# A new start for a four-layer graph kernel: order of the first loads, shape of the weight chunks, who does the one-time work, and the ranks of the matmuls

## The chip, the cores and the metric

The kernel runs on one core of a Trainium2 chip (trn2). The metric is the device time of one execution in microseconds (us), as the median of several runs. The engines are named as the profile names them: PE is the tensor engine (PEld its weight loads), DVE the vector engine, ACT the scalar engine, POOL the general engine, SP the engine that here only starts transfers. ACT can start transfers on a queue of its own as well.

## The reference

There are 128 batches of x with shape [128 nodes, 512 features] in float32, one common matrix adj [128, 128], and four layers. Each ends in a residual sum and a normalization over the 512 features.

```python
x = ln(x + max over m of relu(adj @ x [n] + b_n - (adj@x)[n] + (adj@x)[m]))   # layer 0; both weights are adj
q, k, v = x @ Wq + bq, x @ Wk + bk, x @ Wv + bv                               # layer 1: 8 heads of 64
x = ln(x + softmax(q k^T / 8 + (1 - adj) * -1e9) @ v @ Wo + bo)
h = x @ W;  e = leaky_relu(h a1 [n] + h a2 [m]) * adj                         # layer 2
x = ln(x + elu(softmax(e) @ h + beta * h))
x = ln(x + norm_adj @ (x @ weight) + bias)                                    # layer 3
```

In layer 0 the sum of adj @ x cancels but for a maximum over the features of a row, so one product A = adj @ x, a row maximum R and the bias b give it. Six products of a 128-row batch with a 512 x 512 matrix remain in layers 1 to 3: Q, K, V, Y (Wo), U (W) and Z (weight).

## The kernel before, in words

**Products.** The six products are made for a pair of batches at a time (256 rows), each by seven half-size products in place of eight (`seven_steps` writes the steps, `seven` the code). A product n has four weight combinations nT0 to nT3, made once at the start by subtractions of quarters of the weight (L699), four sums of the moving operand nS1 to nS4 (POOL, L716, for each pair), and the seven products nP1 to nP7 (PE, L737). In the profile px, py and pz are the three PSUM banks of a product: `px_V<-wv_sb,xT` is a half-product of V that reads the plain weight, `py_Q<-SX_V,QT` one that reads a sum and a combination.

**Layers.** For each batch: LD loads x (SP), ST0 takes its statistics (DVE, L640), A is adj @ x (PE, `ps_a`, L854), R the row maximum (DVE). Q0 (ACT), P0 (POOL, a power, L667) and AP0 (ACT, L671 and L672) are the normalization, in which L671 scales the shift and L672 applies scale and shift to 128 x 512 values. MX1 writes the result to a DRAM scratch dx. For batches from 4 on, MX2 reads it back in blocks of 32 rows (`xB`) and TX turns these on DVE into xT, the moving operand of Q, K and V. The first four batches don't go by way of DRAM: PX copies x into the block layout (DVE), PT turns it on PE against an identity (`ps_x`, L909), PTE copies it to xT (DVE). SC are the scores (`ps_s`), MX to SMN the softmax (L975, L981, L990, L995), O the product with v, OE its copy; then Y, the layer's second half; L and E to GE layer 2 (`ps_gT` is the turned mixture of nodes, L1034 its copy gT, on ACT); U, and so to NX, Z and OUT in layer 3.

**One-time work.** BQ scales the bias bq, MASK makes the mask of the softmax, LOG makes W a1 and W a2 (eight DVE products of 128 x 512 with a sum, L602, in one step), ROW a row of biases, NORM the normalized adj of layer 3. The weights come as four chunks of 256 KB each. wq, bq, bk and b0 are loaded from ACT's queue and all others from SP's (the list FETCH). `weight` loads chunks of 128 rows; `turned_weight`, used for Wq, Wk and Wv, loads chunks that land on 32 of the 128 partitions.

**Order.** All of these are entries of a table STEPS. Each has an engine, a cost, the steps that it follows, and the buffers that it takes with the steps that release them (POOLS holds how many buffers there are of a name). `list_order` goes through the table before the program is built and writes out one order. Among the steps that can start on PE it takes the one with the lowest `rank`, which is the batch number plus a constant of the step, the table LAG, less a correction for single pairs, the table LEAD. On other engines `soon` and `rush` put a step ahead. The engines then run their own list in that order, with semaphores between them. So a queue (of ACT, DVE, POOL, SP) is in order: what waits holds up all that stands behind it.

The lines of the profile that are spoken of most are:

```python
                (nc.vector if n in "QK" else nc.gpsimd).tensor_tensor(x, y, z, ALU.subtract)   # L699, nT0 to nT3
...
        return t, [(t[q * S : (q + 1) * S], v[q]) for q in range(Q)]                           # turned_weight
```

Of the kernel before, what the change touches and what calls it, by code (L numbers as in the profile page):

```python
# [172 lines left out]
def normed(b):  # L173
# [12 lines left out]
    "BQ": Step("DVE", 0.2, ("ADJ1", 3.0), batches=first),  # L186
    "MASK": Step("DVE", 0.5, "R", batches=first),
    "ROW": Step("PE", 3.5, "BV", "BO", takes={"ps": ("ROW1",)}, batches=first),
    "ROW1": Step("DVE", 0.7, "ROW", batches=first),
    "LOG": Step("DVE", 5.7, "BETA", "A1", batches=first, port=True),  # L190
    "LOG1a": Step("PE", 0.45, "LOG", takes={"ps": ("LOG2a",)}, batches=first),
    "LOG1b": Step("PE", 0.45, "LOG", takes={"ps": ("LOG2b",)}, batches=first),
    "LOG2a": Step("DVE", 0.65, "LOG1a", batches=first),
    "LOG2b": Step("DVE", 0.65, "LOG1b", batches=first),
    "NORM": Step("DVE", 1.2, "MASK", batches=first, port=True),
    "NORM1": Step("PE", 0.2, "NORM", takes={"ps": ("NORM2",)}, batches=first),
    "NORM2": Step("DVE", 0.3, "NORM1", batches=first),
    "LD": Step("SP", 0.4, ("LD-1", 0.0), ("LD-2", 8.0), takes={"x": ("MX1", "PX")}, dma=(2.55, 0.9)),
    "ST0": Step("DVE", 0.82, "LD", takes={"t0": ("AP0+",)}, rush=40),
    "ADJ": Step("PE", 0.2, ("LD", 2.3), takes={"ps": ("ADJ1",)}, batches=first),  # L200
# [5 lines left out]
    "AP0": Step("ACT", 1.03, "P0+", soon=20, rush=40),  # L206
    "MX1": Step("SP", 0.4, "AP0", ("MX1-1", 0.0), takes={"dx": ("MX2+", "RL")}, dma=(1.55, 0.9), rush=40),

    "PX": Step("DVE", 0.6, "AP0", takes={"xB": ("PT",)}, soon=20, batches=early, port=True, rush=40),
    "PT": Step("PE", 0.5, "PX", takes={"ps": ("PTE",)}, batches=early),  # L210
# [49 lines left out]
    "WK0 WK1 WK2 WK3 WV0 WV1 WV2 WV3 WO0 WO1 WO2 WO3 BV BO W20 W21 W22 W23 A0 A1 BETA W30 W31 W32 W33 B3"  # L260
).split()
for i, name in enumerate(FETCH):
    after = (FETCH[i - 1], 1.0 if i < 8 else 3.0) if i else ("LD@", 2.0)
    STEPS[name] = Step("SP", 0.4, after, batches=first, dma=(2.5, 0.9 if name[0] == "W" else 0.1))
for i in range(4):
    after = ((f"WQ{i - 1}", 0.4),) if i else ()
    STEPS[f"WQ{i}"] = Step("ACT", 0.1, *after, batches=first, dma=(2.5, 0.9))
# [14 lines left out]
def seven_steps(n, sums, needs, weights, pool, out, add=(), turned=False, copy=False, T="POOL"):  # L282

    def step(name, engine, cost, *after, takes=(), soon=0.0):
        after = [(sums if a[0] == "S" else n) + a if isinstance(a, str) else a[0] for a in after]
        STEPS[n + name] = Step(engine, cost, *after, takes=takes, soon=soon, batches=even if sums == "X" else paired)  # L290

    needs = [(a,) for a in needs]
    for i in range(4):
        after = [f"{n}T{i - 1}"] if i else weights
        cost = 1.34 if T == "POOL" else 0.75
        STEPS[f"{n}T{i}"] = Step(T, cost, *after, batches=first, port=True)
    parts = [n + p for p in ("P1", "P2", "P3", "P4", "P5", "P6", "P7")]
    parts += [f"{sums}S{i}" for i in (1, 2, 3, 4)] + [n + "F1"] * (sums != "X")
    for s in STEPS.values():
        s.takes = {  # L300
            p: (*r, *(q + "+" for q in parts)) if p == pool else r for p, r in s.takes.items()
        }
    last = {"R2": add, "U3": turned, "C21": True}
    last = n + next(k for k in last if last[k])
    c = 0.893 if turned else 0.866
    step("P1", "PE", c, "S1", *needs, takes={
        "ps": (n + "C11",), "u": (last,), **({"uL": (n + "C21",)} if turned else {}), **out
    })
    step("P6", "PE", c, "S2", "P1", (n + "T2@",), takes={"ps": (n + "C21",)})
    step("P5", "PE", c, "S1", "P6", takes={"ps": (n + "C12",)})  # L310
    step("P2", "PE", c, "u", *(("uL",) if turned else ()))
    step("P7", "PE", c, "S3", "U2")
    step("P4", "PE", c, "U3", (n + "T3@",))
    step("P3", "PE", c, "S4", "C22")
    added, low = "u", "uL" if turned else "u"
    if add:
        step("R1", "POOL", 0.75, "u", *((a,) for a in add), soon=20)
        step("R2", "POOL", 1.3, "R1", soon=20)
        added = low = "R2"
    step("u", "ACT", 0.42 if turned else 0.3, "P1", soon=20)  # L320
    if turned:
        step("uL", "ACT", 0.42, "P1", soon=19)
    step("U2", "DVE", 0.37, "P6", "R1" if add else "u", soon=20)
    step("U3", "DVE", 0.37, "P7", added, soon=20)
    if copy or turned:
        step("C11", "ACT", 0.42 if turned else 0.3, "P2", soon=10)
    else:
        step("C11", "DVE", 0.37, "P2", "R1", soon=10)
    step("C21", "DVE", 0.37, "P4", low, soon=10)
    step("C22", "DVE", 0.37, "U3", "P5", soon=10)  # L330
    step("C12", "DVE", 0.37, "U2", "P3", soon=10)
    return [n + c + "+" for c in ("C11", "C12", "C21", "C22")]
# [6 lines left out]
for n, needs, letters in (  # L339
# [4 lines left out]
    "Q": seven_steps("Q", "X", ["TX+", "PTE+", "BQ@"], ["WQ3"], "xT", {"qT": ("SC+",)},  # L344
                     turned=True, T="DVE"),
    "K": seven_steps("K", "X", ["TX+", "PTE+", "BQ@"], ["WK3"], "xT", {"kT": ("SC+",)},
# [3 lines left out]
    "U": seven_steps("U", "U", ["GE+"], ["LOG", "W23"], "gT", {"x3": ("OUT+",)}, copy=True),  # L350
    "Z": seven_steps("Z", "Z", ["NE+"], ["W33"], "nx", {}, add=["C3+"]),
}
for n, need, weights, end, out in (
# [16 lines left out]
    "A": 0.692, "QP4": 9.305, "QP6": 13.674, "KP4": 14.013, "QP1": 14.257, "VP6": 14.264,  # L370
    "QP7": 14.272, "KP7": 14.275, "QP2": 14.757, "KP6": 14.810, "QP5": 16.139,
    "KP1": 16.167, "SC": 16.245, "QP3": 16.292, "KP5": 16.483, "KP2": 16.726, "KP3": 16.957,
    "VP1": 17.469, "VP7": 17.505, "VP2": 17.717, "VP4": 17.842, "VP3": 17.872,
    "VP5": 17.926, "YP4": 18.786, "YP5": 19.034, "O": 20.374, "YP3": 21.316, "YP1": 21.809,
    "YF1": 21.819, "YP2": 21.908, "YP6": 21.936, "YP7": 22.056, "E": 22.106, "UF1": 22.207,
    "YF0": 22.911, "BT": 23.043, "UP1": 23.223, "GT": 23.299, "UP4": 23.974, "UP5": 24.264,
    "UP3": 24.731, "UP2": 24.753, "UP6": 24.814, "UP7": 24.920, "UF0": 25.326,
    "ZP7": 25.453, "ZF0": 25.880, "NX": 25.925, "ZP4": 26.433, "ZP2": 26.459, "ZP6": 26.533,
    "ZP1": 27.158, "ZP3": 27.371, "ZP5": 27.563, "ZF1": 28.500,
}  # L380

LEAD = {
    "V55": -0.01, "NX59": 0.02, "GT60": -2.5, "V60": 0.06, "BT61": 0.07, "Z61": -1.43,
    "BT62": -0.59, "GT63": 1.52, "NX63": -0.85, "A4": 3.8, "O0": 1.06, "O1": -0.73, "GT2": 0.02,
    "V1": -0.26,
# [6 lines left out]
def rank(name, b):  # L392
    if name not in LAG:
        return -1.0
    stage = name[0] if name[1:2] in "PF" else name
    if name in ("SC", "O") and b in BOTH:
        b |= 1
    return b + LAG[name] - LEAD.get(f"{stage}{b // 2}", 0.0)


@with_exitstack
def kernel(
# [61 lines left out]
    nc.scalar.dma_start(out=b0_sb, in_=b0.rearrange("(p o) -> p o", o=1))  # L464
# [3 lines left out]
    def LD(b):  # L468
        xs[b] = buf("x", [P, D], b)
        nc.sync.dma_start(out=xs[b], in_=x[b])  # L470
# [5 lines left out]
    def turned_weight(w, name):  # L476

        t = const.tile([P, C, D], F32, tag=name, name=name)
        v = w.rearrange("(q c s) f -> q s c f", q=Q, s=S)
        return t, [(t[q * S : (q + 1) * S], v[q]) for q in range(Q)]  # L480
# [8 lines left out]
    def row(v, offset, size, name):  # L489
# [19 lines left out]
        *wk_parts, *wv_parts, *wo_parts, bv_part, bo_part, *w2_parts, *a_parts, beta_part, *w3_parts,  # L509
# [10 lines left out]
    for part in (bq_part, bk_part):  # L520
        fetch(nc.scalar, part)
# [18 lines left out]
    prep = {}  # L540

# [15 lines left out]
    def NORM():  # L557
# [5 lines left out]
        nc.vector.tensor_scalar(dis, deg, TINY, None, op0=ALU.max)  # L563
        nc.gpsimd.tensor_tensor(dis, dis, neg_half, ALU.pow)
        nc.vector.tensor_tensor(dis, dis, pos, ALU.mult)
# [30 lines left out]
    def LOG():  # L596
        nc.vector.tensor_scalar(beta_id, ident, beta_c, None, op0=ALU.mult)
        for i in range(2):
            col = prep[i] = tiny(f"wa_col{i}", 0, C)
            for c in range(C):  # L600
                prod = buf("m", [P, D], f"prod_{i}_{c}")
                nc.vector.scalar_tensor_tensor(  # L602
                    prod,
                    w2_sb[:, c, :],
                    1.0,
                    a_bc[i],
                    op0=ALU.mult,
                    op1=ALU.mult,
                    accum_out=col[:, c : c + 1],
                )  # L610
# [58 lines left out]
    def apply(dst, src, layer, b):  # L669
        shift, scale = off[layer, b // 2][:, b % 2], rstd[layer, b // 2][:, b % 2]  # L670
        nc.scalar.activation(shift, shift, AF.Identity, scale=scale)  # L671
# [226 lines left out]
    def PX(b):  # L898
        xB[b] = buf("xB", [P, Q, P], b)
        nc.vector.tensor_copy(  # L900
            xB[b].rearrange("p c (q s) -> p c q s", s=S),
            xs[b].rearrange("p (q c s) -> p c q s", q=Q, s=S),
        )
# [307 lines left out]
    def OUT(b):  # L1211
# [5 lines left out]
        LD, ST0, A, R, P0, AP0, MX1, PX, PT, PTE, MX2, RL, C1, TX, SC, M0, M, SM1, EXP, SMR, SMN, MS1, MS2, TS, O, OE,  # L1217
        Y1, P1, AP1, L, E, EZ, E1, EE, E2, BT, BE, GT, GE, U1, UE, U2, UP, U3, P2, AP2, NX, NE,
        C3, Z1, P3, AP3, OUT,
    )}  # L1220
    for name in FETCH:
        do[name] = lambda b, part=parts[name]: fetch(nc.sync, part)
    for f in (ADJ, ADJ1, BQ, MASK, NORM, NORM1, NORM2, ROW, ROW1, LOG):
        do[f.__name__] = lambda b, f=f: f()
# [3 lines left out]
    for i in range(4):  # L1228
        do[f"WQ{i}"] = lambda b, i=i: fetch(nc.scalar, wq_parts[i])
# [47 lines left out]
```

## Time and profile before

| | |
|---|---|
| median of three runs | 3055.86 us (3053.38 to 3056.80) |
| span of the profiled execution | 3055.6 us (its own time is not given apart from it) |
| PE busy, idle | 3021.9 us, 33.7 us |
| DVE, ACT, POOL busy | 2350.8, 2215.0, 1624.7 us |
| first product with a weight (px_Q) starts | 24.52 us |
| first half-product of K starts | 46.49 us |
| 600 to 2900 us: PE busy | 2297.58 of 2300 us |

A row of the timeline reads: start and duration in us, engine, line, operation, output and inputs by the program's names, tile, shape, how many alike were put together, and in brackets the idle time of the engine just before it with what ended it. A row of the windows reads: the stretch in us and its length, busy us of each engine with the number of instructions, then the granted clock of PE (1.00 is full speed), the mean busy share of the 16 DMA engines, and what they moved in GB/s. The chain of waits follows the work that ended last back to its releasers.

### The profile page before, as it was taken

Reading aid. Unit: us, or ns where it says so; the run is one execution under the profiler, and the core shown is the slowest. Engines: PE = TensorE matmul, PEld = TensorE weight load, DVE = VectorE, ACT = ScalarE, POOL = GpSimd, SP = SyncE. Lnnn points to the kernel's source line nnn. Section 1 sums busy time; section 2 is a strip of 40 time slices with the busy share of each in tenths; the row PEclk is TensorE's granted clock in tenths of the full one; section 3 lists DMA queues with packets and bytes.
Section 4 is the critical chain, followed back from the end, with each engine's and each line's share of the span. In section 5 each row is a group of like instructions: output and inputs, shape, how many; then the busy total and the mean of one; then the engine's idle time right before and its main releaser. Section 6 shows DMA issues by size and latency. Waiting matters only on the chain.

```text
span 3055.6 us, 61911 instructions
## 1 busy us (share of the span) xinstructions
PE 3021.9 (99%) x21062; PEld 2706.8 (89%) x21062; DVE 2350.8 (77%) x5379; ACT 2215.0 (72%) x7240; POOL 1624.7 (53%) x1907
## 2 busy tenths in 40 slices
PE   7999999999999999999999999999999999999998
PEld 5888988988989989989889899898898898999987
DVE  6878777787787787877777877878778777777774
ACT  4677777777777776777777777777777777667675
POOL 4336555455455555554554655545545545556544
PEclk8999999999999999999999999999999999999999
DMA  7523333233233332332332323323323333223221
GB/s 198 179 87 124 89 107 111 85 116 104 84 118 98 97 114 88 111 108 83 118 102 91 117 88 107 111 87 115 104 84 118 98 97 109 86 77 97 70 84 38
DMA packets 235276, 313.19 MB, mean 102 GB/s; under 512 B 27729, under 2 KB 157649, under 8 KB 234961
## 3 DMA queue, kind: packets, MB, share of 16 engines
q1 hardware_dynamic: 233184, 308.19, 31.9%
q8 instruction: 167, 2.74, 0.4%
q10 hardware_dynamic: 1776, 1.05, 0.2%
q14 instruction: 149, 1.21, 0.1%
HBM read 174.92 MB, written 134.22 MB: 101 GB/s over the span
## 4 chain that ended last, share of the span: by engine, by line
PE 94%; DVE 3%; DMA 2%; ACT 1%; issue 0%; SPq 0%; POOL 0%; ACTq 0%; POOLq 0%; DVEq 0%
PE py_Q L737 6%; PE py_K L737 5%; PE py_U L737 5%; PE py_Y L737 5%; PE py_V L737 5%; PE py_Z L737 5%; PE ps_s L945 4%; PE pz_Q L737 4%; PE px_K L737 4%; PE pz_K L737 4%; PE ps_o L1024 4%; PE ps_nx L1181 4%; PE px_Q L737 4%; PE ps_gT L1130 4%; PE px_Z L737 4%; PE pz_V L737 4%
## 5 line engine op out<-in xcount | busy, mean ns | idle before, releaser
L1195 POOL TENSOR_TENSOR x<-x,b_bc 128x512 f32<-128x512 f32 x128 | 162.8, 1273 | 601.7 <-PE ps_nx L1181 601.6
L672 ACT ACTIVATE x<-x,off,rstd 128x512 f32<-128x512 f32 x512 | 416.8, 814 | 17.1
L981 ACT ACTIVATE s<-s,mx 128x128 f32<-128x128 f32 x1024 | 396.1, 390 | 36.7 <-DVE mx L975 36.6
L640 DVE BATCH_NORM_STATS2 st<-x 128x6 f32<-128x512 f32 x512 | 346.6, 677 | 13.9 <-POOL x L1162 7.7
L995 ACT ACTIVATE s<-s,sm 128x128 f32<-128x128 f32 x1024 | 313.3, 389 | 18.5 <-DVE sm L990 7.8
L667 POOL TENSOR_TENSOR rstd<-rstd,neg_half 128x2 f32<-128x2 f32 (+1 forms) x265 | 182.3, 688 | 149.9 <-ACT rstd L653 149.7
L1162 POOL TENSOR_TENSOR x<-x,x 128x512 f32<-128x512 f32 x128 | 163.2, 1275 | 142.4 <-DVE rs L1108 75.4
L716 POOL TENSOR_TENSOR SX_V<-xT 128x256 f32<-128x256 f32 x128 | 93.7, 732 | 272.2 <-PE py_Y L737 243.8
L1034 ACT COPY nx<-ps_nx 128x512 f32<-128x512 f32 x128 | 74.9, 585 | 215.9 <-PE ps_nx L1181 215.6
L1066 DVE SCALAR_TENSOR_TENSOR junk<-x,wa_bc 128x512 bf16<-128x512 f32 x256 | 207.1, 809 | 14.8 <-ACT x L672 4.0
L796 DVE TENSOR_TENSOR x<-py_U,u_U 128x256 f32<-128x256 f32 x183 | 77.6, 424 | 151.8 <-PE py_U L737 151.3
L981 ACT ACTIVATION_READ_ACCUMULATOR s<-s,mx 128x1 f32 x1024 | 193.5, 189 | 0.0
L959 DVE TENSOR_TENSOR s<-ps_s,mask 128x512 f32<-128x512 f32 x256 | 169.1, 682 | 9.3 <-DMA dp<-s 5.8
L896 POOL TENSOR_TENSOR x<-x,bo_bc 128x512 f32<-128x512 f32 x128 | 160.3, 1274 | 14.5 <-DVE bo_bc L593 8.1
L716 POOL TENSOR_TENSOR S_U<-gT 128x256 f32<-128x256 f32 x122 | 93.0, 762 | 128.8 <-ACT gT L1034 128.6
L1016 DVE STREAM_TRANSPOSE sB<-sB 128x1024 f32<-128x1024 f32 x128 | 157.9, 1234 | 0.8 <-DMA sB<-dp 0.8
L737 PEld LDWEIGHTS px_K<-xT,wk_sb 128*128 128x128 f32 x1024 | 133.8, 192 | 27.3 <-issue 23.6
L671 ACT ACTIVATE off<-off,rstd 128x1 f32<-128x1 f32 x512 | 145.6, 284 | 15.4 <-POOL rstd L667 15.2
L975 DVE TENSOR_REDUCE mx<-s 128x8 f32<-128x1024 f32 x128 | 153.5, 1199 | 0.3
L945 PE MATMUL ps_s<-kT,qT 64*128 64x128 f32 x2048 | 148.8, 285 | 0.0
L945 PEld LDWEIGHTS ps_s<-kT,qT 64*128 64x128 f32 x2048 | 124.3, 187 | 23.4 <-issue 23.1
L854 PE MATMUL ps_a<-x,adjT 128*128 128x512 f32 x256 | 134.4, 609 | 6.5 <-DMA x<-in_x 6.5
(190 smaller groups left out, 9151.1 us busy)
## 6 DMA issues: line engine op xcount, KB each, us to landing
dp<-s SPq DMA_DIRECT2D x128, 512.0 KB, 2.9
sB<-dp SPq DMA_DIRECT2D x512, 128.0 KB, 3.1
x<-in_x SPq DMA_DIRECT2D x128, 256.0 KB, 3.4
dx<-x SPq DMA_DIRECT2D x128, 256.0 KB, 4.4
x<-dx SPq DMA_DIRECT2D x64, 512.0 KB, 4.0
out_x<-x SPq DMA_DIRECT2D x128, 256.0 KB, 2.0
xB<-dx SPq DMA_DIRECT2D x496, 64.0 KB, 2.0
wo_sb<-in_L_gnn_Wo SPq DMA_DIRECT2D x5, 256.0 KB, 3.7
```

What stands on the lines that cost most here:

```text
L640: nc.vector.bn_stats(st, t)
L667: nc.gpsimd.tensor_tensor(r, r, neg_half.to_broadcast([P, r.shape[1]]), ALU.pow)
L672: nc.scalar.activation(dst, src, AF.Identity, bias=shift, scale=scale)
L716: nc.gpsimd.tensor_tensor(s[:, i], x, y, op)
L737: nc.tensor.matmul(to, lhsT=one, rhs=two, start=(new and k == 0), stop=(k == 1), skip_group_check=True,)
L945: nc.tensor.matmul(scores[b][par][:, c, :], lhsT=qT[b][rows, c, cols], rhs=kT[b][rows, c, cols], start=True, stop=True,)
L959: nc.vector.tensor_tensor(by_head(probs[b])[:, par * C : (par + 1) * C], scores[b][par].rearrange("p h (q s) -> p h q s", s=S), mask.rearr ...
L981: nc.scalar.activation(s[:, :, h], s[:, :, h], AF.Exp, bias=mx[:, h : h + 1], accum_out=sums[b][:, h : h + 1],)
L995: nc.scalar.activation(s[:, :, h], s[:, :, h], AF.Identity, scale=sm[:, h : h + 1])
L1066: nc.vector.scalar_tensor_tensor(junk, x2[b][:, b % 2], 1.0, wa_bc[i], op0=ALU.mult, op1=ALU.mult, accum_out=s12[b][:, i : i + 1],)
L1162: nc.gpsimd.tensor_tensor(t, t, x2.pop(b)[:, b % 2], ALU.add)
L1195: nc.gpsimd.tensor_tensor(t, t, b3_bc, ALU.add)
```

## The change

What it does, part by part:

- **First loads.** x_0 is loaded from ACT's queue with b0 behind it, and x_1 from SP's. The chunks of wq and the biases bq and bk move from ACT's queue to SP's, where the order is now adj, x_1, wq (4), bq, x_2, x_3, wk (4), bk, wv (4), dx_0, dx_1, wo (2), x_4, and so on. A load of x is released by MX1 alone.
- **Weight chunks.** A chunk of `turned_weight` is now one c for all q and s, so that it lands on all 128 partitions (2 KB each); before it was one q, on 32 partitions (4 times 2 KB each).
- **Layout copy.** PX is gone. For batches 0 to 3 ACT applies the normalization to x twice: once straight into the block layout (AB), then in place (AP0).
- **Identity turns.** 44 turns of the identity into a scores bank that nobody reads: WU0 (12) ahead of adj's turn, WU1 (14) after A of batch 1, WU2 (10) after A of batch 3, WU3 (8) after PT of batch 1.
- **One-time work.** LOG is split into one small step and eight, NORM into three with its power on POOL, BQ waits for its own load and MASK stands behind PTE; Q's and K's combinations follow other steps.
- **Ranks.** LAG has new constants, with two further tables, EARLY for the batches below 8 and LATE for those from 120; LEAD is gone.

```diff
-    "BQ": Step("DVE", 0.2, ("ADJ1", 3.0), batches=first),
-    "MASK": Step("DVE", 0.5, "R", batches=first),
+    "BQ": Step("DVE", 0.2, "BQL", batches=first, rush=60),
+    "MASK": Step("DVE", 0.5, "PTE+", batches=first),
...
-    "LOG": Step("DVE", 5.7, "BETA", "A1", batches=first, port=True),
-    "LOG1a": Step("PE", 0.45, "LOG", takes={"ps": ("LOG2a",)}, batches=first),
-    "LOG1b": Step("PE", 0.45, "LOG", takes={"ps": ("LOG2b",)}, batches=first),
+    "LOG": Step("DVE", 0.2, "BETA", batches=first),
+    **{f"LOG{i}": Step("DVE", 0.72, "BETA", f"LOG{i - 1}" if i else "LOG", batches=first, port=True)
+       for i in range(8)},
+    "LOG1a": Step("PE", 0.45, "LOG3", takes={"ps": ("LOG2a",)}, batches=first),
+    "LOG1b": Step("PE", 0.45, "LOG7", takes={"ps": ("LOG2b",)}, batches=first),
...
-    "NORM": Step("DVE", 1.2, "MASK", batches=first, port=True),
-    "NORM1": Step("PE", 0.2, "NORM", takes={"ps": ("NORM2",)}, batches=first),
+    "NORM": Step("DVE", 0.7, "QC12", batches=first),
+    "NORMP": Step("POOL", 0.58, "NORM", batches=first),
+    "NORMA": Step("DVE", 0.5, "NORMP", batches=first, port=True),
+    "NORM1": Step("PE", 0.2, "NORMA", takes={"ps": ("NORM2",)}, batches=first),
...
-    "LD": Step("SP", 0.4, ("LD-1", 0.0), ("LD-2", 8.0), takes={"x": ("MX1", "PX")}, dma=(2.55, 0.9)),
+    "LD": Step("SP", 0.4, ("LD-1", 0.0), ("LD-2", 2.0), takes={"x": ("MX1",)}, dma=(2.55, 0.9)),
...
-    "ADJ": Step("PE", 0.2, ("LD", 2.3), takes={"ps": ("ADJ1",)}, batches=first),
+    "WU0": Step("PE", 2.4, takes={"sc": ("WU0",)}, batches=first),
+    "WU1": Step("PE", 1.6, ("A", 0.0), takes={"sc": ("WU1",)}, batches=lambda b: b == 1),
+    "WU2": Step("PE", 1.1, ("A", 0.0), takes={"sc": ("WU2",)}, batches=lambda b: b == 3),
+    "WU3": Step("PE", 0.9, ("PT", 0.0), takes={"sc": ("WU3",)}, batches=lambda b: b == 1),
+    "ADJ": Step("PE", 0.2, ("LD", 2.3), "WU0", takes={"ps": ("ADJ1",)}, batches=first),
...
-    "AP0": Step("ACT", 1.03, "P0+", soon=20, rush=40),
+    "AB": Step("ACT", 1.1, "P0+", takes={"xB": ("PT",)}, soon=20, batches=early, rush=80),
+    "AP0": Step("ACT", 1.03, "P0+", "AB", soon=20, rush=40),
...
-    "PX": Step("DVE", 0.6, "AP0", takes={"xB": ("PT",)}, soon=20, batches=early, port=True, rush=40),
-    "PT": Step("PE", 0.5, "PX", takes={"ps": ("PTE",)}, batches=early),
+    "PT": Step("PE", 0.5, "AB", takes={"ps": ("PTE",)}, batches=early),
...
-    "WK0 WK1 WK2 WK3 WV0 WV1 WV2 WV3 WO0 WO1 WO2 WO3 BV BO W20 W21 W22 W23 A0 A1 BETA W30 W31 W32 W33 B3"
+    "WQ0 WQ1 WQ2 WQ3 BQL WK0 WK1 WK2 WK3 BKL WV0 WV1 WV2 WV3 WO0 WO1 WO2 WO3 BV BO W20 W21 W22 W23 A0 A1 BETA W30 W31 W32 W33 B3"
...
-    step("P1", "PE", c, "S1", *needs, takes={
+    step("P1", "PE", c, *([] if sums == "X" else ["S1"]), *needs, takes={
...
-    "Q": seven_steps("Q", "X", ["TX+", "PTE+", "BQ@"], ["WQ3"], "xT", {"qT": ("SC+",)},
+    "Q": seven_steps("Q", "X", ["TX+", "PTE+", "BQ@"], ["WQ3", "P0"], "xT", {"qT": ("SC+",)},
...
-    "K": seven_steps("K", "X", ["TX+", "PTE+", "BQ@"], ["WK3"], "xT", {"kT": ("SC+",)},
+    "K": seven_steps("K", "X", ["TX+", "PTE+", "BKL@"], ["WK3", "XS4"], "xT", {"kT": ("SC+",)},
...
-    stage = name[0] if name[1:2] in "PF" else name
-    if name in ("SC", "O") and b in BOTH:
-        b |= 1
-    return b + LAG[name] - LEAD.get(f"{stage}{b // 2}", 0.0)
+    lag = (EARLY if b < 8 else LATE if b >= 120 else LAG)[name]
+    return (b | 1 if name in ("SC", "O") else b) + lag
...
-        nc.sync.dma_start(out=xs[b], in_=x[b])
+        (nc.sync if b else nc.scalar).dma_start(out=xs[b], in_=x[b])
+        if b == 0:
+            nc.scalar.dma_start(out=b0_sb, in_=b0.rearrange("(p o) -> p o", o=1))
...
-        v = w.rearrange("(q c s) f -> q s c f", q=Q, s=S)
-        return t, [(t[q * S : (q + 1) * S], v[q]) for q in range(Q)]
+        v = w.rearrange("(q c s) f -> c q s f", q=Q, s=S)
+        return t, [(t[:, c, :], v[c]) for c in range(C)]
...
-    for part in (bq_part, bk_part):
-        fetch(nc.scalar, part)
...
+    def WU(n):
+        def step(b):
+            ps = psum.tile([P, C, P], F32, tag="sc", name=f"ps_warm_{b}", bufs=POOLS["sc"])
+            for i in range(n):
+                nc.tensor.transpose(ps[:, i % C, :], ident, ident)
+        return step
...
+    def LOG0(i, c):
+        if c == 0:
+            prep[i] = tiny(f"wa_col{i}", 0, C)
+        nc.vector.scalar_tensor_tensor(
+            buf("m", [P, D], f"prod_{i}_{c}"),
+            w2_sb[:, c, :],
+            1.0,
+            a_bc[i],
+            op0=ALU.mult,
+            op1=ALU.mult,
+            accum_out=prep[i][:, c : c + 1],
+        )
...
-    def PX(b):
+    def AB(b):
         xB[b] = buf("xB", [P, Q, P], b)
-        nc.vector.tensor_copy(
+        shift, scale = off[0, b // 2][:, b % 2], rstd[0, b // 2][:, b % 2]
+        nc.scalar.activation(shift, shift, AF.Identity, scale=scale)
+        nc.scalar.activation(
             xB[b].rearrange("p c (q s) -> p c q s", s=S),
             xs[b].rearrange("p (q c s) -> p c q s", q=Q, s=S),
+            AF.Identity, bias=shift, scale=scale,
         )
```

The three rank tables in full are of no use to a reader; as examples, KP2 goes from 16.726 to 18.942, UF1 from 22.207 to 37.454 and ZF0 from 25.880 to 8.142 in LAG.

## The prediction

> **What bounds the kernel now.** I read the page's rows of busy time first, then the windows (after the stretch: busy us of each engine, TensorE's granted clock, DMA share, GB/s), then TensorE's timeline with its waits, last the chain.
>
> ```profile
> span 3055.6 us, 61911 instructions
> PE 3021.9 (99%) x21062; PEld 2706.8 (89%) x21062; DVE 2350.8 (77%) x5379; ACT 2215.0 (72%) x7240; POOL 1624.7 (53%) x1907
> ...
> PEclk8999999999999999999999999999999999999999
> ```
> TensorE works in all but 33.7 us of the span.
> ```profile
> 0.00:10.00 10.00, 4.20 (x5) 1.29 (x5) 4.50 (x15) 1.99 (x5) 0.81 (x9) 1.00 0.78 162
> 10.00:20.00 10.00, 2.40 (x3) 0.64 (x3) 2.30 (x8) 2.64 (x7) 1.23 (x2) 0.60 1.07 227
> 20.00:30.00 10.00, 7.04 (x25) 4.66 (x25) 8.18 (x19) 4.02 (x12) 5.08 (x7) 0.72 0.69 232
> 30.00:40.00 10.00, 7.96 (x36) 6.27 (x37) 8.98 (x13) 2.78 (x11) 6.25 (x7) 0.83 0.76 224
> ...
> 600.00:2900.00 2300.00, 2297.58 (x16188) 2072.21 (x16188) 1789.72 (x4094) 1691.66 (x5525) 1260.22 (x1478) 1.00 0.32 100
> ```
> From 600 to 2900 us only 2.4 of 2300 us are idle, so nothing can be won there; the same row shows what could be lost. The loss lies in the first 40 us, where the clock was 0.60 to 0.83 besides.
> ```profile
> 16.87 2.07 PE L854 MATMUL ps_a<-x,adjT 128*128 128x512 f32 x2 [5.18 <-DMA x<-in_x]
> ...
> 24.52 1.57 PE L737 MATMUL px_Q<-xT,wq_sb 128*128 128x128 f32 x8
> 25.93 1.03 PE L737 MATMUL px_V<-wv_sb,xT 128*128 128x256 f32 x4
> ...
> 46.49 1.05 PE L737 MATMUL px_K<-xT,wk_sb 128*128 128x128 f32 x8
> ...
> 89.54 1.22 PE L737 MATMUL py_Q<-SX_V,QT 128*128 128x128 f32 x8 [2.31 <-DVE qT L789]
> ```
> The start waits for x_2 behind the weights; the first weight product starts at 24.52. Up to 46.49 TensorE does 8 A (ps_a, 0.86 each warm), 4 turns of x (0.45), 7 half-products of Q (0.89), 5 of V (0.87) and adjT (0.2), 19.45 us at full clock. So **the start loses 46.49 - 19.45 = 27.0 us**. A second loss is at 89.54: 2.31 us of idling and, with clocks of 0.61 and 0.54 in the two windows behind it, about 1.7 more. The DVE timeline ahead of it shows eight LOG products (L602) in one block from 82.29 to 88.98, with qT behind them. The tail after the last matmul is 7.2 us.
>
> **The change part by part.** The profiled execution's span, 3055.6, stands 0.26 below the median of 3055.86, which I ignore beside a spread of 3.4.
>
> *Multiset.* Matmuls stay 10,672, plus 44 idle turns of the identity; runs of one matmul form go from 270 to 268. So TensorE's full-clock work is unchanged, and only stalls and clock differ.
>
> *Weight chunks over 128 partitions (decides most).* What rows show of the two shapes:
> ```profile
> 6.00:8.00 2.00, 2.00 (x4) 0.61 (x2) 1.47 (x4) 0.00 (x0) 0.00 (x0) 1.00 1.07 200
> 84.00:86.00 2.00, 2.00 (x9) 1.15 (x8) 1.90 (x7) 1.66 (x8) 0.00 (x0) 1.00 1.05 396
> ```
> With all engines full, chunks on 32 partitions move 200 GB/s and loads on 128 partitions 396. By these rows the new chunk of 256 KB takes 0.66 us instead of 1.3. [...] Four engines move 4 x 396/16 = 99 GB/s: 2.65 us a chunk, 12 chunks 32 us on the same four engines, and whatever stands behind them on SP waits there. [...]
>
> *Start, four engines.* SP now issues adj, x_1, wq0-3, bq, x_2, x_3, wk0-3, bk, wv0-3, dx_0, dx_1, wo0, wo1, x_4. adj and x_1 are through near 4.4; wq lands at 7.1, 9.8, 12.4, 15.1; x_2 and x_3 at 16.1 and 16.8 (each about 0.66 on 16 engines); wk ends at 27.5; wv1 lands at 33.2 and wv3 at 38.6; dx_0 39.3, x_4 42.05. DVE's BQ and the four QT sums (0.69 each, L699 of the chain) need all of wq and stand ahead of PTE, done 19.5. TensorE: A2 and A3 at low clock to 19.6, the turns to 21.8, px_Q at 22.8 (before 24.52). Next in its order is px_V, which needs wv0 and wv1: **it stops from 23.7 to 33.2**. Then Q, V and two turns go on at low clock, A4 starts at 43.0 with x_4, and A5 ends at 44.8. By then 6 A, 4 turns, 7 Q, 2 V and adjT, 15.1 us of full-clock work, are done: loss 29.7, **+2.7** on before.
>
> *Queues moved past.* ACT loses six DMA issues and gains one (x_0); SP gets five more ahead of x_2. On ACT the copy of px_V (u_V) now stands ahead of AB2 and AB3, so they start at 34.2 and end near 37.5; the turns of x_2 and x_3 wait for them, ahead of A4's 43.0, hence no further cost. On POOL the four VT sums wait for wv3 at 38.6 and hold S sums of the second pair only. MX1 alone now releases x: x_4 takes the buffer that dx_0 frees, itself behind wv at 39.3, and is ready 2.75 later, after dx_1, wo0 and wo1, as counted above.
>
> *Start, sixteen engines.* wq is there by 7 and the path is x_2, R, AB, PT, PTE: px_Q near 14.5, A5 ends at 25.4 to 26.4: loss about 11, **-16**.
>
> *AB on ACT for PX on DVE.* Takes four copies (3.2 us in sum) from DVE; ACT pays 0.81 and 0.28 a batch, the rows of L672 and L671, in a stretch where its windows show 2.6 to 4 of 10 us busy. Counted in the walk. AP0 comes after AB and only dx waits for it, which no product needs before TX of batch 4. LD 0 on the ACT queue starts as early as before; b0 behind it is first read after A0.
>
> *44 turns.* At most 0.28 each (the eight of 20.77 took 2.25 at low clock), 12 us in groups of 12, 14, 10 and 8, all in stretches in which TensorE waits for x_0, x_2, AB and PTE. Cost 0; if all these covers went, 0.11 to 0.28 each, 5 to 12 us. As for the clock, the row has 0.60 to 0.72 from 10 to 30 us. [...] In the four-engine case px_V waits anyhow; in the other the difference is about 1.7 us, within its range.
>
> *LOG in eight pieces, MASK and NORM later.* The 6.7 us block goes, and the 2.31 + 1.7 behind it: **-4.0**. What is late next there is DVE itself, 18.8 of 20 us busy from 80 to 100, so up to 2 could come back. In exchange DVE at 43 to 48 has st_4, st_5, R4, R5, deg and two KT sums ahead of V's and K's additions: **+1.5** (0 to 3). NORM's pow on POOL is one 0.69 piece and only NORM1 waits for it.
>
> *Ranks.* EARLY and LATE order the two ends, LAG the middle. LATE ends pair 126 whole ahead of 127: **-0.5** (-1.4 to 0) of the tail. EARLY puts O_0 20.3 us of matmuls behind SC_0, the softmax chain needing 18.2, and similar tight places: **+1** (0 to 3). In the middle the order is almost that of before, with one difference: px_U comes 3 matmul steps (2.7 us) behind ps_gT instead of 6.
> ```profile
> 1429.27 2.45 ACT L995 ACTIVATE s<-s,sm 128x128 f32<-128x128 f32 x8
> 1431.62 0.56 ACT L1034 COPY gT<-ps_gT 128x512 f32<-128x512 f32 x1
> ...
> 1432.26 0.73 POOL L716 TENSOR_TENSOR S_U<-gT 128x256 f32<-128x256 f32 x1 [2.41 <-ACT gT L1034]
> ...
> 1435.27 1.03 PE L737 MATMUL px_U<-w_sb,gT 128*128 128x256 f32 x4
> ```
> The copy waited for ACT's softmax block, S_U ended at 1432.99 and px_U came 2.3 us later; walked in the new order the slack is about 1.1. Cost **0**; below nothing is excluded, since only 2.4 us are idle there, and above nothing is the third case.
>
> Sum, four engines: 3055.6 + 2.7 + 1.5 - 4.0 - 0.5 + 1.0 = 3056.3, with the 0.26 **3056.5** (3049 to 3064).
>
> **The rivals.** *Sixteen engines:* -16 - 4.0 - 0.5, +1 to +2: **3038** (3033 to 3045). For it: the row of 396 GB/s for loads on 128 partitions. [...] *The middle stalls (slower):* in the order S_U then px_U the slack of 1.1 us is exceeded whenever ACT starts its 2.45 us block just before ps_gT ends. From a delay of 1.1 on, TensorE waits once a pair; a mean of 0.3 over some 55 pairs is +16: **3072** (3062 to 3085). For it: ACT is 1691.66 of 2300 us busy, and blocks of eight go uninterrupted. Against it: before has places with like slack and idles 2.4 us in 2300. *It does not do what it says:* the early loads are late behind slow chunks; that is the forecast itself, and why a prologue made to be shorter is here not.
>
> **How the numbers follow.** Four engines 0.70, sixteen 0.15, stalls in the middle 0.13, others 0.02. 0.2% (6.1 us) is about what a measurement of this kernel tells from no change: bounds 3049.7 and 3062.0. Faster: all of sixteen and 0.10 of the first, 0.25. Slower: all of stalls, 0.14 of the first and the others, 0.25 together. Same: 0.50. The range 3038 to 3070 leaves out half of the second and of the third case and little else, about 0.17. The likeliest case alone holds 3049 to 3064.
>
> **What would show it.** Right: weight chunks landing about 2.65 us apart; DMA share near 0.25 to 0.4 up to 38 us; TensorE idle over 8 us ahead of the first px_V, released by wv_sb; no idle of 2 us behind LOG; the 600 to 2900 window still above 2297 busy. Wrong: px_V within 2 us of px_Q and px_Q before 17 (sixteen engines); or over 10 us of idle ahead of px_U or S_U between 600 and 2900, released by gT (stalls).

## The result, and the profile after

The changed kernel takes 3093.68 us (median of 4 runs, 3091.88 to 3096.09) against 3056.33 us: a ratio of 1.0123, interval 1.0109 to 1.0137. It is slower by 37 us. The forecast of 3056.5 was wrong, and so was its range up to 3070. The profiled execution of the changed kernel took 3091.88 us, the fastest of the four; its span is 3090.0 us, 34.4 longer than the span before. So the traces show 34.4 us of the loss, and the start that they show is that of the quickest of the four.

The page first, in the same rows as before:

```profile
span 3090.0 us, 61891 instructions
...
PE 3040.0 (98%) x21106; PEld 2706.6 (88%) x21106; DVE 2369.1 (77%) x5375; ACT 2207.7 (71%) x7244; POOL 1636.0 (53%) x1907
```

TensorE idles for 50.0 us where it idled for 33.7. Now the windows of the changed kernel (stretch, busy us of each engine, granted clock, DMA share, GB/s):

```profile
0.00:10.00 10.00, 6.55 (x31) 4.91 (x31) 3.54 (x9) 3.16 (x9) 1.52 (x10) 1.00 0.36 112
10.00:20.00 10.00, 2.31 (x3) 1.17 (x4) 2.42 (x5) 3.00 (x5) 0.00 (x0) 0.57 0.41 131
20.00:30.00 10.00, 5.37 (x36) 4.15 (x34) 6.54 (x13) 2.17 (x9) 3.48 (x5) 0.84 0.29 99
30.00:40.00 10.00, 6.71 (x31) 5.84 (x32) 0.88 (x2) 2.86 (x7) 0.00 (x0) 0.56 0.52 174
...
600.00:2900.00 2300.00, 2283.03 (x15954) 2040.01 (x15954) 1786.28 (x4043) 1663.48 (x5456) 1249.88 (x1455) 1.00 0.31 99
```

Two things are to be read here. The start is no shorter, and between 20 and 30 us the sixteen DMA engines were busy to 0.29 and moved 99 GB/s. While only weights move (18 to 20 us, for one) the share is 0.26, where it is 1.12 with the old form of the chunks (12 to 16 us of e4, below). That is about a quarter, as much as four of the sixteen engines give when they are busy all the time; no view names the engines. And the last row, which had 2297.58 us of TensorE in 2300, has 2283.03, with 234 matmuls fewer (15,954 against 16,188). The loss is in the middle.

TensorE's timeline of the start:

```profile
17.69 3.78 PE L892 MATMUL ps_a<-x,adjT 128*128 128x512 f32 x4 [8.29 <-DMA x<-in_x]
...
24.31 1.06 PE L775 MATMUL px_Q<-xT,wq_sb 128*128 128x128 f32 x8
31.59 1.20 PE L775 MATMUL px_V<-wv_sb,xT 128*128 128x256 f32 x2 [6.21 <-DMA wv_sb<-in_L_gnn_Wv]
34.48 1.22 PE L775 MATMUL px_V<-wv_sb,xT 128*128 128x256 f32 x2 [1.70 <-DMA wo_sb<-in_L_gnn_Wo]
...
44.18 1.88 PE L892 MATMUL ps_a<-x,adjT 128*128 128x512 f32 x4
```

The second px_V waits for the second chunk of wv; its row names wo, but the releaser is inferred, and the same row of e3 names wv_sb. This is the walk of the prediction to within 2 us (table further below). So where are the 34 us? The product of v (`ps_o`) of one and the same pair of batches can be found in both timelines, here of batches 6 and 7 and of batches 118 and 119, first before, then after:

```profile
231.87 1.97 PE L1024 MATMUL ps_o<-sB,v 128*64 128x128 f32 x32
2842.64 1.97 PE L1024 MATMUL ps_o<-sB,v 128*64 128x128 f32 x32
```
```profile
232.03 1.97 PE L1065 MATMUL ps_o<-sB,v 128*64 128x128 f32 x32
2877.46 1.97 PE L1065 MATMUL ps_o<-sB,v 128*64 128x128 f32 x32
```

At the first point the two profiles are 0.16 us apart, at the second 34.82. In 56 pairs 34.7 us are lost, 0.62 us in each on the mean, and the end adds -0.4. The median distance from one pair to the next is 46.69 us before and 47.35 after.

TensorE's table of waits from 600 to 2900 us, which in the changed kernel has a single row (engine and tile that waited, for what, us in total, times, longest), names the place:

```profile
PE py_Z L775 <- DVE x L834: 16.7, 49, 0.4
```

The kernel before has one row there too, another one:

```profile
PE pz_V L737 <- DVE v L796: 2.4, 4, 1.1
```

One such place in the changed kernel, first TensorE's timeline, then that of DVE:

```profile
1420.31 1.13 PE L775 MATMUL px_Z<-w_sb,nx 128*128 128x256 f32 x4
1421.27 1.03 PE L775 MATMUL py_Z<-ZT,S_Z 128*128 128x256 f32 x4
1422.14 1.03 PE L775 MATMUL px_Z<-w_sb,nx 128*128 128x256 f32 x4
1423.00 1.05 PE L1171 MATMUL ps_gT<-bT,x 128*128 128x128 f32 x8
1424.39 1.13 PE L775 MATMUL py_Z<-ZT,S_Z 128*128 128x256 f32 x4 [0.34 <-DVE x L834]
1425.36 1.03 PE L775 MATMUL px_V<-wv_sb,xT 128*128 128x256 f32 x4
```
```profile
1421.18 1.21 DVE L1016 TENSOR_REDUCE mx<-s 128x8 f32<-128x1024 f32 x1
1422.31 0.88 DVE L1199 SCALAR_TENSOR_TENSOR x<-m,x 128x512 f32<-128x512 f32 x1
1423.12 0.68 DVE L677 BATCH_NORM_STATS2 st<-x 128x6 f32<-128x512 f32 x1
1423.83 0.18 DVE L678 BATCH_NORM_AGGREGATE mv<-st 128x2 f32<-128x6 f32 x1
1423.93 0.41 DVE L834 TENSOR_TENSOR x<-py_Z,x 128x256 f32<-128x256 f32 x1
```

The second half-product py_Z (step ZP7) adds onto the bank that the DVE sum `x<-py_Z,x` (step ZU2) has to read first. That sum stands behind a maximum, an addition and statistics of other layers on DVE and ends at 1424.34. ZP7's turn was at 1423.89. In the kernel before, the same place reads:

```profile
1407.19 1.05 PE L1130 MATMUL ps_gT<-bT,x 128*128 128x128 f32 x8
1408.08 1.03 PE L737 MATMUL px_V<-wv_sb,xT 128*128 128x256 f32 x4
1408.94 1.03 PE L737 MATMUL py_V<-VT,SX_V 128*128 128x256 f32 x4
1409.81 1.03 PE L737 MATMUL py_Z<-ZT,S_Z 128*128 128x256 f32 x4
```
```profile
1408.13 0.40 DVE L796 TENSOR_TENSOR x<-py_Z,x 128x256 f32<-128x256 f32 x1
```

There the sum ended at 1408.53, and ZP7 came at 1409.81, behind two half-products of V: 1.28 us of slack. The new ranks (ZP7 from 25.453 to 1.702) put ZP7 ahead of these two, 1.73 us sooner. 1.28 - 1.73 = -0.45 us. On DVE nothing moved: from the start of px_Z to the start of the sum it is 3.64 us before and 3.62 after. The row shows 0.34 idle; the rest stands beside it, since TensorE also loses the overlap of one product with the next (the step from ps_gT to py_Z is 1.39 long, not 0.89, and that from py_Z to px_V 0.97, not 0.86).

### The profile page after: what moved, and what is told of

The parts are those of the page before. It is cut to its first block, busy times and chain, and to the rows that moved or that the text cites. A ratio compares the mean times of both kernels' runs of the same rounds, so it can differ in the third digit from the quotient of the medians.

```text
span 3090.0 us, 61891 instructions
## 1 busy us (share of the span) xinstructions
PE 3040.0 (98%) x21106; PEld 2706.6 (88%) x21106; DVE 2369.1 (77%) x5375; ACT 2207.7 (71%) x7244; POOL 1636.0 (53%) x1907
## 4 chain that ended last, share of the span: by engine, by line
PE 80%; DVE 14%; ACT 2%; issue 1%; SPq 1%; DMA 1%; POOL 0%; ACTq 0%; POOLq 0%; DVEq 0%
PE py_Q L775 5%; PE py_K L775 5%; PE py_U L775 5%; PE py_V L775 5%; PE py_Y L775 5%; PE py_Z L775 4%; PE ps_nx L1222 4%; PE pz_Q L775 4%; PE px_Q L775 4%; PE pz_K L775 4%; PE px_K L775 4%; PE pz_V L775 3%; PE pz_U L775 3%; PE px_U L775 3%; PE px_V L775 3%; PE pz_Y L775 3%
## 5 line engine op out<-in xcount | busy, mean ns | idle before, releaser
L775 PEld LDWEIGHTS py_Q<-SX_V,QT 128*128 128x128 f32 x1024 | 125.8, 193 | 31.8 <-issue 29.8
L775 PE MATMUL py_Z<-ZT,S_Z 128*128 128x256 f32 x488 | 131.3, 392 | 19.9 <-DVE x L834 19.9
L775 PE MATMUL px_V<-wv_sb,xT 128*128 128x256 f32 x512 | 133.0, 382 | 8.7 <-DMA wv_sb<-in_L_gnn_Wv 6.2
```

The costliest lines, as they stand in the source:

```text
L775: nc.tensor.matmul(to, lhsT=one, rhs=two, start=(new and k == 0), stop=(k == 1), skip_group_check=True,)
```

## The experiments

All are the changed kernel or the kernel before with the edit shown; times are medians, with the kernel before at 3055.6 to 3055.9 in the same sessions. "The written order" is what `list_order` gives; `moved` is a function put around it.

**e1: ZP7 later.** Only the place of ZP7 in the changed kernel.

```diff
+def moved(order):
+    names = [(name, b) for _, name, b in order]
+    for b in range(0, 128, 2):
+        if ("ZP7", b) not in names:
+            continue
+        i = names.index(("ZP7", b))
+        near = names[i + 1 : names.index(("ZU3", b))]
+        sixth = [k for k in near if k[0] == "VP6"]
+        if sixth:
+            names.insert(names.index(sixth[0]), names.pop(i))
+    return [(0.0, *k) for k in names]
...
-        for _, name, b in list_order(STEPS, rank, POOLS, B):
+        for _, name, b in moved(list_order(STEPS, rank, POOLS, B)):
```

> The changed kernel with one step moved in the written order: of each pair, ZP7 (the second half-product py_Z) stands behind VP1 and VP6, as in the kernel before, not ahead of them. Theory (P7 comes 1.73 us sooner than in the kernel before and so 0.45 us ahead of the DVE sum of py_Z that it waits for): the pair's period goes from 47.35 back to 46.69 us, no wait of py_Z for DVE is left, and 52 pairs of 0.66 give back 34 us: 3059 us (3054 to 3063). Rival (the new ranks cost elsewhere too, by matmuls that take longer after changes of form): less than 20 us come back, 3074 or more. Rival (the new start is what costs): nothing comes back, 3093.

Measured: 3072.12 us, ratio 1.0052 (1.0040 to 1.0065). 21.6 of the expected 34 us came back, near the border of the first rival. The wait of py_Z is gone from the table. What stays beside e3 (below) is 0.21 us a pair in the traces (46.87 from one pair to the next on the mean of batches 6 to 118, and 46.67 in e3), and the timeline shows it as a step that is too long, without a wait beside it:

```profile
1421.57 1.03 PE L788 MATMUL py_V<-VT,SX_V 128*128 128x256 f32 x4
1422.54 1.10 PE L788 MATMUL pz_Z<-w_sb,S_Z 128*128 128x256 f32 x4
1423.48 1.03 PE L788 MATMUL px_V<-wv_sb,xT 128*128 128x256 f32 x4
```
```profile
1420.85 1.24 DVE L1070 STREAM_TRANSPOSE sB<-sB 128x1024 f32<-128x1024 f32 x1
1422.01 0.39 DVE L847 TENSOR_TENSOR x<-pz_Z,x 128x256 f32<-128x256 f32 x1
```

From py_V to pz_Z it is 0.97 us and not 0.86, and the next step 0.94. pz_Z adds onto the bank that a DVE sum has to read first, and this sum ends at 1422.40, behind a transpose of 1.24. On the mean of 900 to 2300 us the two steps cost 0.18 us more a pair than in e3, some 10 us in 56 pairs. With ZP7 moved alone, the products of Z behind it are too close to their own sums. So moving this one step doesn't restore the old order, and e1 by itself leaves room for the first rival; e2 and e3 decide.

**e2: the kernel before with ZP7 earlier.** The same kind of function moves ZP7 ahead of VP1; nothing else of the change is in it.

> The kernel before with one step moved: ZP7 of each pair stands ahead of VP1 and VP6, straight behind ps_gT, as in the changed kernel. Nothing else of the change is in it. Theory (the distance of P7 from the DVE sum is enough by itself): a wait of 0.34 us in each pair, period 47.35, 58 pairs by 0.66 us: 3094 us (3088 to 3097). Rival (it needs the other ranks of the change as well): 3056 to 3060.

Measured: 3101.64 us, ratio 1.0150 (1.0136 to 1.0164). The one step suffices; it costs 46 us where 38 were expected. The table of waits has the same row as the changed kernel, 16.8 us in 49 times; the other 8 us fit two of Z's later steps, as in e1 (from py_Z<-ZT,nx to the next it is 0.97 on the mean of 900 to 2300 us, not 0.87, and from pz_Z 0.90).

```profile
PE py_Z L750 <- DVE x L809: 16.8, 49, 0.4
```

**e3: the sum earlier on DVE.** TensorE's order is that of the change; on DVE the statistics (step U3) go behind ZU2.

```diff
+        i = names.index(("ZU2", b))
+        near = [k for k in names[i - 4 : i] if k[0] == "U3"]
+        if near:
+            names.insert(i, names.pop(names.index(near[0])))
```

> The changed kernel with PE's order untouched; on DVE the sum that P7 waits for (ZU2, x<-py_Z) stands ahead of the statistics of layer 2 (U3, 0.68 and 0.18 us) in each pair. Theory (P7 is late only because ZU2 is queued behind that block on DVE): ZU2 ends 0.86 us sooner, 0.4 us ahead of P7's turn; no wait is left, period 46.7 to 46.8, 3059 us (3054 to 3066). Rival (P7 waits for something else that ends at the same time, such as the matmul P6 or POOL's sum R1): most of the wait stays, 3080 or more.

Measured: 3060.23 us (18 runs), ratio 1.0016 (1.0009 to 1.0023). 33.5 of the 37 us are back, with ZP7 as early as in the change. The DVE and PE timelines of this kernel at such a place:

```profile
1412.40 0.89 DVE L1211 SCALAR_TENSOR_TENSOR x<-m,x 128x512 f32<-128x512 f32 x1
1413.20 0.41 DVE L846 TENSOR_TENSOR x<-py_Z,x 128x256 f32<-128x256 f32 x1
1413.54 0.68 DVE L689 BATCH_NORM_STATS2 st<-x 128x6 f32<-128x512 f32 x1
```
```profile
1413.08 1.05 PE L1183 MATMUL ps_gT<-bT,x 128*128 128x128 f32 x8
1413.97 1.03 PE L787 MATMUL py_Z<-ZT,S_Z 128*128 128x256 f32 x4
```

The sum ends at 1413.61, and py_Z starts at 1413.97 without waiting. From one pair to the next it is 46.75 us (median), where it was 47.35. So P7 waited for nothing but ZU2's place in DVE's queue. What the rest of the change costs is 4.7 us in medians.

**e4: the old form of the weight chunks.** e1 with

```diff
-        v = w.rearrange("(q c s) f -> c q s f", q=Q, s=S)
-        return t, [(t[:, c, :], v[c]) for c in range(C)]
+        v = w.rearrange("(q c s) f -> q s c f", q=Q, s=S)
+        return t, [(t[q * S : (q + 1) * S], v[q]) for q in range(Q)]
```

> The changed kernel with ZP7 moved as in e1 and, besides, the chunks of Wq, Wk and Wv in the old form (32 partitions of 4 times 2 KB, 32 outermost in the source). Theory (the new form runs on four of the sixteen DMA engines, and px_V waits for wv behind eight such chunks): a chunk takes 1.3 instead of 2.5 us, wv is there by 22, px_V starts near 22 and not at 31.6 and 34.5, A4 near 33 and not at 44.2: 8 to 12 us less than e1, 3049 us (3044 to 3053). Rival (the start is bound by something else, such as SP's issuing or the chain of statistics): within 3 us of e1.

Measured: 3060.80 us (21 runs), 11.3 less than e1. The windows and the timeline show the start as expected:

```profile
12.00:16.00 4.00, 3.92 (x24) 2.57 (x23) 3.64 (x7) 2.51 (x5) 0.00 (x0) 1.00 1.12 201
```
```profile
23.02 2.05 PE L788 MATMUL px_V<-wv_sb,xT 128*128 128x256 f32 x4 [5.15 <-DMA wv_sb<-in_L_gnn_Wv]
...
33.80 1.88 PE L905 MATMUL ps_a<-x,adjT 128*128 128x512 f32 x4
```

201 GB/s at a share of 1.12 with chunks on 32 partitions, against 99 GB/s at 0.29 with chunks on 128 (20 to 30 us of the changed kernel). A4 comes at 33.80 and not at 44.18.

**e5: the kernel before with the new form of the chunks** (the two lines of e4 the other way round).

> The kernel before with the new form of the chunks of Wq, Wk and Wv and nothing else of the change. Theory (twelve chunks on four of sixteen DMA engines, 2.5 us each, some 30 us in all): px_V can start only when wv is there, near 34 us and not at 25.9, DMA share near 0.3 from 12 to 30 us: slower by 4 to 11 us, 3063. Rival (all sixteen engines, or a start bound by the statistics): within 2 us of the kernel before.

Measured: 3069.40 us, ratio 1.0047 (1.0034 to 1.0059): 13.6 us slower, more than expected. The mechanism was right, the first victim another one: not px_V, but A2, whose x stands behind weights on the same queue.

```profile
27.17 2.08 PE L854 MATMUL ps_a<-x,adjT 128*128 128x512 f32 x2 [15.94 <-DMA x<-in_x]
...
36.92 1.03 PE L737 MATMUL px_V<-wv_sb,xT 128*128 128x256 f32 x4
```

**e6: both mended.** e3's DVE order and e4's chunks in the changed kernel.

> The changed kernel with two edits: the DVE order of e3 (the sum for P7 ahead of the statistics) and the old form of the weight chunks as in e4. Theory (the two losses are independent: 33 us in the pairs, 11.3 us in the start): 3060.2 - 11.3 = 3049 us (3046 to 3052), faster than both kernels. Rival (part of the shorter start is lost again in the first pairs, which wait for something else): 3053 or more.

Measured: 3048.98 us (20 runs), ratio 0.9978 (0.9972 to 0.9985). The two losses add up as expected, and without them the change is a gain of 6.8 us.

**e7: wv ahead of wk** in FETCH, otherwise e6.

> As e6, with wv ahead of wk in SP's list. Theory (the start's next bound is the load of wv, for which px_V waited 5.2 us in e4): px_V starts near 18 and not at 23.0, A4 near 29: 4 to 6 us less than e6, 3044 us (3042 to 3048). Rival (DVE's KT sums or dx and x_4 behind the weights take the place of that wait): within 2 us of e6.

Measured: 3061.49 us (18 runs), 12.5 more than e6. px_V did start at 16.96. But FETCH feeds the planner, which wrote another order: in this one TensorE waits 4.85 us for x at 93.61 and runs at a clock of 0.83 from 80 to 100 us. It is busy for 14.05 of these 20 us, in e6 for 18.90; the rest of the 12.5 isn't placed.

```profile
93.61 3.75 PE L904 MATMUL ps_a<-x,adjT 128*128 128x512 f32 x4 [4.85 <-DMA x<-in_x]
```

**e8: four turns in place of 44** (`range(1)` in place of `range(n)`), otherwise e6.

> As e6, with four turns of the identity in place of 44 (one for each group); the order is the same. Theory (the turns lie in waits and do not hold the clock): within 1.5 us of e6, granted clock from 8 to 16 us not lower than in e6. Rival (they keep the clock up in this shorter start): the A of batches 2 and 3 and the first turns of x run at half clock (0.5 to 0.6 from 12 to 16 us), 2 to 4 us more than e6. Rival (they are in the way): 1 to 3 us less than e6.

Measured: 3046.78 us (7 runs), ratio 0.9971 (0.9961 to 0.9982), 2.2 us less than e6. The intervals of the two ratios overlap a little, so the gain isn't sure; its size is that of the second rival (they are in the way), and more than the theory allowed. The pace did change. A of batches 2 and 3 in e6, and in e8:

```profile
12.01 1.88 PE L904 MATMUL ps_a<-x,adjT 128*128 128x512 f32 x4
```
```profile
10.96 3.68 PE L904 MATMUL ps_a<-x,adjT 128*128 128x512 f32 x4 [0.73 <-DMA x<-in_x]
```

With 14 turns ahead of them the same four matmuls ran in half the time, 1.88 us for 3.68. Only these durations tell: the windows have a granted clock of 1.00 from 8 to 16 us in both runs. The other runs with the old chunks agree, 2.23 and 1.90 us with all turns (e4, e7) and 3.78 with four (e10). It bought nothing, since the turns themselves take at least what they save (the 14 take 2.00 us in e6, the four matmuls behind them 1.80 less than in e8): A2 starts later by 1.05 us in e6, px_Q starts at 16.57 in e6 and at 15.97 in e8, and then px_V waits for wv and starts at 22.29 and at 22.27.

**e9: the kernel before with LOG in pieces**, as in the diff of the change, but that the small step still waits for A1 too.

> The kernel before with LOG as one small step and eight pieces, as in the changed kernel; nothing else of the change, though the written order near that place shifts with it. Theory (the 6.7 us block on DVE cost 4.0 us at 89.54): no wait of 2 us of py_Q for qT between 80 and 95 us, 2 to 4 us less: 3052.5 us. Rival (DVE is so full there that the time comes back in other waits): within 1.5 us of the kernel before.

Measured: 3061.32 us (21 runs), ratio 1.0018 (1.0011 to 1.0024): slower by 5.4, which neither theory nor rival foresaw. From 60 to 100 us the only wait left is 0.4 us, where 2.3 stood before. But TensorE is busy for 92.79 us of the next 100, before for 98.50:

```profile
80.00:100.00 20.00, 19.57 (x151) 16.23 (x151) 19.51 (x47) 12.53 (x45) 6.19 (x5) 1.00 0.80 244
100.00:200.00 100.00, 92.79 (x680) 80.24 (x679) 76.45 (x174) 72.04 (x267) 35.24 (x44) 1.00 0.37 116
```

What was won by 100 us is lost by 200. The order near that place shifted too, so this run doesn't say how much of it is DVE's load and how much is the order.

**e10: wv ahead of wk, the order kept.** e8, with the loads of wv and wk exchanged in SP's list alone.

```diff
+    slots = [i for i, k in enumerate(names) if k[0][:2] in ("WK", "WV", "BK")]
+    loads = [names[i] for i in slots]
+    for i, k in zip(slots, [k for k in loads if k[0][:2] == "WV"] + [k for k in loads if k[0][:2] != "WV"]):
+        names[i] = k
```

> As e8 (sum for P7 earlier, old chunks, four turns), with wv ahead of wk in SP's list and every other list exactly as in e8. Theory (in e7 it was the order that the planner wrote anew for the other load that lost the time, with A waiting 4.9 us for x at 93.6; the earlier wv itself is a gain): px_V near 17, 2 to 5 us less than e8: 3043 us. Rival (KT, ahead of the first qT sums on DVE and now waiting for a later wk, gives the time back): within 1 us of e8.

Measured: 3045.09 us (3040.55 to 3045.47, 5 runs), ratio 0.9962 (0.9949 to 0.9974): 10.8 us less than the kernel before, 1.7 less than e8 by medians, with overlapping intervals: between the theory (2 to 5) and the rival (within 1). The profiled execution is the one of 3040.55, 4.5 below the median, so the other four lose somewhere what the lines below show as won. px_V starts at 17.23 and A4 at 27.22 and not at 33.09; KT takes back 1.16 us ahead of py_Q.

```profile
17.23 1.03 PE L791 MATMUL px_V<-wv_sb,xT 128*128 128x256 f32 x4
...
22.73 1.13 PE L791 MATMUL py_Q<-SX_V,QT 128*128 128x128 f32 x8 [1.16 <-DVE qT L843]
...
27.22 1.88 PE L908 MATMUL ps_a<-x,adjT 128*128 128x512 f32 x4
```

So e7's loss was the order and not the load. This version has the lowest median here.

**e11: four turns with the new chunks** (e3 with the edit of e8).

> As e3 (new chunks, the sum for P7 ahead of the statistics), with four turns of the identity in place of 44. Theory of the prediction (on four engines TensorE waits for wv in any case, so the turns cost and bring nothing): within 1.5 us of e3's 3060.2. Rival (they are in the way here as in e6, where leaving 40 out brought 2.2): 3058. Rival (they hold the clock): 3062.

Measured: 3059.89 us (21 runs) against e3's 3060.23. In the start with the new chunks the turns cost and bring nothing that these runs can tell.

## Why the prediction was wrong, point by point

| step | forecast | measured |
|---|---|---|
| weight chunk on four engines | 2.65 us, 99 GB/s | 93 to 102 GB/s while only weights move (2.6 to 2.8 us a chunk), share 0.26 to 0.27 |
| px_Q starts | 22.8 us | 24.31 |
| px_V starts | 33.2 | 31.59, second half 34.48 |
| A4 starts | 43.0 | 44.18 |
| all effects up to batches 6 and 7 | +1.2 | +0.2 |
| the middle | 0 | +34.7 |
| tail | -0.5 | -0.4 |

- **The step that failed is "Ranks", in the sentence that in the middle the order is almost that of before, with one difference, px_U behind ps_gT, at a cost of 0.** There was a second difference, ZP7 two half-products sooner: a wait of 0.34 us and a lost overlap, 0.66 us together in the median pair. e3, which undoes the wait alone, gives 33.5 us back. (Of the 34.7 in the table about 2 are not of this kind: they lie between batches 6 and 10, where the pairs of e3 are as long as those of the change, 47.9 and 47.5 us against 46.7 and 46.8 before.) It could have been read without a run: the slack of 1.28 us is in the trace of before (1408.53 and 1409.81), and the shift of 1.73 is in the two orders. I walked one link out of all whose distance had shrunk and took it for the whole.
- **The slower rival** had the right kind of loss (a wait once a pair, in the middle) at less than half its size (+16, range to 3085), and the wrong place: a copy on ACT ahead of px_U. No wait of px_U stands in the table. That its mean wait of 0.3 us is close to the 0.34 of idle time is luck, since it was taken of another link. In size it lacked the lost overlap: 0.62 us a pair for 0.34 of idle time.
- **The weight chunks held.** No row of before shows that a new chunk runs on four engines; I took it so, and the 2.65 us a chunk and the +2.7 of the sum rest on it. The runs showed 93 to 102 GB/s at a share of 0.26 to 0.27, and not the 396 GB/s of the row for other loads on 128 partitions; e4 and e5 price the new form at 11.3 and 13.6 us. That the start nearly broke even all the same is due to the rest of the change taken together, which e6 shows as a gain of 6.8 once the chunks and ZU2 are mended. The runs don't split it between AB, the order of loads and the ranks; the split of LOG alone was a loss in e9.
- **LOG at -4.0** stood for what is visible at 89.54. The wait vanished in the change and in e9, but e9 gave it all back by 200 us. The +0.2 at batches 6 and 7 is a sum, and it is of the quickest of four executions: there A of batches 0 and 1 took 1.98 us, in e1 and e3 with the same start 3.78, and in these two the product of v of batches 6 and 7 comes at 233.05 and 235.21. The runs don't split the sum between LOG, the crowding of DVE at 43 to 48 and the early order.
- **The turns at 0** were right for this start: 3059.89 us with four of them against 3060.23 with all (e11, e3). Whether they keep up the pace no row of before showed; in the shorter start of e6 and e8 A2 and A3 took 1.88 us with all turns and 3.68 with four, a difference of 1.80, where the prediction has about 1.7. In the changed kernel TensorE waits 8.29 us for x between the turns and A2, and there A2 and A3 took 3.78.
- **The rest.** In e3, whose ranks are those of the change, 4.7 us remain against the kernel before. The forecast for all but ZP7 was +0.7, so these terms were 4 us too kind; which of them, the runs don't show.

## What to carry to other kernels

When an order is rewritten in a loop that is 99% busy, list every link whose distance between producer and consumer shrank, and subtract the shrinking from the slack that the trace shows; one link below zero is paid in every turn of the loop. A consumer that must come earlier can often be served by moving its producer ahead of unrelated work on the producer's queue (e3), which here beat moving the consumer back (e1). Change the data path and the written order apart from each other: the same load order cost 12.5 us with a new plan (e7) and nothing, perhaps a gain of 1.7, with the old one (e10).

## What the runs showed of the hardware

- A wait of about 0.1 us has no row: the idle time starts only once the matmul before has fully ended (in the changed kernel ps_gT ends at 1424.05, and the 0.34 of py_Z runs from there to 1424.39), and successive products overlap by 0.17 us (py_V lasts 1.03 and steps by 0.86). Such waits show as a longer step (0.97) and a longer next product (1.10 for 1.03); some 10 of the 12 us by which e1 stays above e3 are of this kind. (The ends of matmuls are modelled in the profile.)
- SP took longer to issue wk in the new form: 7.35 us for its four chunks in the changed kernel (from 10.22 on), 2.72 in the old form (e4) and 3.46 in the kernel before. It issued dx_0 and dx_1 from 28.68 on, not from 15.52 (e4). The four chunks of wq, of the new form too and third in its list, took 2.62. Why an issue takes longer there, and how much of the delay is SP's and not the slower transfers', the runs don't show.
